# A selective-scan block with a Sinkhorn mixing tail: gate one state earlier, make-up factor 1.1, conv taps one tick later, mixing from the end of the first Sinkhorn chain

## The chip, the cores and the metric

The kernel runs on one core of one Trainium2 chip. The metric is the time of one execution on the device in microseconds (us). Each profile is one execution of the program taken by the hardware profiler. The engines are named as the profile does: PE (TensorE, matmuls; PEld its weight loads), DVE (VectorE), ACT (ScalarE), POOL (GpSimd), SP (SyncE, which issues DMAs).

## The reference

The computation is one layer with adaptive layer norms: a selective state-space block, then a residual mixing of four streams. Cut to what matters:

```python
mod = (silu(c) @ wmod)                                # six rows per batch: sa, ca, ga, sb, cb, gb
h = layernorm(x) * (1 + ca) + sa                      # x: 4 x 512 x 1024
x = x + ga * attn(h)
h = layernorm(x) * (1 + cb) + sb
x = x + gb * ffn(h)

def attn(h):                                          # DIN 2048, N 16 states, R 64, K 4
    x, z = split(h @ in_proj_w)
    xc = silu(causal_conv4(x))                        # 4 taps along the sequence
    dt_r, Bm, Cm = (rmsnorm of three slices of xc @ x_proj_w)
    dt = softplus(dt_r @ dt_proj_w + dt_bias)
    h_t = exp(dt_t * A) * h_(t-1) + dt_t * B_t * x_t  # for 2048 channels x 16 states
    y_t = sum over states of h_t * C_t
    return ((y + D * xc) * silu(z)) @ out_proj_w

def ffn(x):                                           # 4 streams of 256
    H_res = sinkhorn_log(x_norm @ W_res + base)       # 4 x 4 per position, 50 iterations
    H_res = (1 - g) * I + g * H_res
    x_pre = sum_n x_n * H_pre_n                       # H_pre, H_post: softmaxes
    return H_res @ x_streams + H_post * (x_pre @ W_branch)
```

## The kernel before

**Blocks, quads, states.** The 2,048 positions are eight blocks k of 256 (a batch and a half of it). The 2,048 channels are four quads q of four 128-channel chunks. The main loop runs over k, q and the 16 states n: 512 steps of `step`, with six ticks each. In one step VectorE runs two scans (L1160, two chunks each, `tensor_tensor_scan` along the positions) on the present state, and two sums (L1146) that add the previous state's h times C to `acc`, one for each half of the positions. ScalarE computes the decays `da` (L1125) for the next step, into the one buffer that each half has. GpSimd computes the inputs `w` (L1111, the u of the quad times B) two steps ahead, into three buffers (`emit_w`; L1116 adds the carried state in the second half of a batch). TensorE transposes the scanned states of the previous step into PSUM (`hq`, L1136, eight transposes into two banks), and does the dense products in between.

**Order.** The loops are under a manual schedule: every engine executes in the order in which the program emits. Generators (`spawn`) emit the rest of the work between the ticks: a generator that yields a number is continued that many ticks later, one that yields "v" at the next gap of VectorE (`gap`, one per tick). Dense products stand in one queue per block (`paced`): x (`product_x`, L616), z (`product_z`, L664), out (`product_out` of the block before, L845) and the projection to dt, B and C (`product_bc`, L697). At every tick the queue issues the share of its matmuls that is due; when it has been held up, it may issue at most MAKE_UP (1.2) times the pace until it has caught up.

**Convolution.** Behind the eight matmuls of a chunk, `product_x` lets ScalarE do the last tap with the bias (L625, `xc`), waits TAP_LAG (3) ticks, and gives VectorE three more taps (L632, 128 x 256 each), each in a gap of its own. The product's PSUM bank (four of the kind `mm`) is held until the last tap.

**Gate.** When a quad is done, `gate_quad` multiplies `acc` by silu(z) on GpSimd (L914, 128 x 1024), transposes the result on TensorE (L929, `py`), copies it on ScalarE into `y` (L936) and marks `done`: `product_out` waits for all four y of its block, the z product two quads on and the `acc` of the quad two on wait for the gate. It is spawned at state 2 of the next quad. Since `product_out` of a block needs the y of its quad 3, it starts in quad 0 of the next block. Its results are transposed (`pr`) and added to x on VectorE (L899, `xr`).

**Sinkhorn chains.** After block 7 the logits of 16 tiles (of 128 positions) are there, first of 14 (`early`), and of the last two (`late`, tiles 14 and 15) somewhat later. The 50 iterations are six small VectorE operations each (`iteration`, L187 to L200), with a renewal of the kernel now and then (`renew`). Chain 0 takes tiles 0 to 7 and chain 1 tiles 8 to 13; when the logits of the late tiles are ready, chain 1 takes them along (its operations become 128 wide instead of 96), noting in `behind` at which iteration. The two chains alternate operation by operation. `end` (L224, L226) writes a chain's mixing coefficients. After both ends the late tiles still lack as many iterations as chain 1 had done before they joined (`chain_late`). The branch product (x_pre @ W_branch, `branch_*`) runs on ScalarE, TensorE and GpSimd beside the chains: its last stage copies with a scale (L1317, `yn`, three buffers) and adds on GpSimd (L1319, L1320).

**Mixing.** For each of 16 tiles `mix_products` makes ten diagonal matrices on ScalarE (L1275), with which TensorE makes ten products (L1341, two instructions each in the profile): all of streams 0 and 1 (`oa`) and two of stream 2 (`ob`); ScalarE starts stream 3 (L1339). `mix_rest` adds the other five terms on VectorE (L1352), multiplies by gb (L1356, L1358), adds x1 on GpSimd (L1359) and stores (L1360). Tile i's products are emitted ahead of tile i-1's rest, and two operations of `chain_late` go between the VectorE operations of a tile; at tile 14 what is left of the chain is emitted at once.

## Time and profile before

| | us |
|---|---|
| runs (3): median, lowest, highest | 2532.35, 2531.55, 2533.06 |
| the profiled execution, its own time | 2531.71 |
| its span | 2529.9 |
| busy: PE, PEld, DVE, ACT, POOL | 2340.1, 1961.1, 2289.9, 1700.7, 1803.9 |
| granted clock of TensorE, mean | 0.965 |

The span divides into a prologue (to 126 us), eight blocks (they begin at 126, 423, 691, 960, 1231, 1498, 1766 and 2033), the end of block 7 with the chains (2292 to 2443) and the mixing (2443 to 2530). A row of the profile's groups gives the line, the engine, the operation, the tiles (out<-in) with their shapes, then the total busy time and the mean in ns of one instruction, then the idle time of the engine ahead of it and what ended it. In a timeline, a run of like instructions is one row: start and duration in us, what ran, how many, and in brackets the idle time before it with its releaser. The ends of consecutive instructions on one engine overlap by about 0.1 us, so the cost of one is its distance to the next start.

### The profile page before, as it was taken

The page shows a single profiled execution, that of the slowest core. Times are in us where ns is not written, and L with a number is a line of the kernel's source. Part 1 is how long each engine was busy: PE and PEld are TensorE (multiplying, and loading weights), DVE is VectorE, ACT ScalarE, POOL GpSimd, SP SyncE. Part 2 cuts the span into 40 slices and gives each one's busy share as a digit, 9 for nine tenths or more (in the row PEclk, how much of TensorE's full clock was granted, in tenths as well). Part 3 has the DMA queues.
Part 4 walks back from the last instruction along what each step waited for, and adds up shares of the span by engine and source line. Part 5 has one row for each costly group of instructions (what it writes and reads, how often), then busy time and mean ns, then how long its engine had stood idle before and what let it go on. Part 6 is the DMA issues. An engine that isn't in the chain of part 4 may idle for free.

```text
span 2529.9 us, 38513 instructions
## 1 busy us (share of the span) xinstructions
PE 2340.1 (92%) x13224; PEld 1961.1 (78%) x13224; DVE 2289.9 (91%) x3539; ACT 1700.7 (67%) x3775; POOL 1803.9 (71%) x1199
## 2 busy tenths in 40 slices
PE   8999989999999999999999999999999999885578
PEld 5766577888888888888788878888888877774567
DVE  2289998999899998999899999999999999988988
ACT  2366577676867686767777786768776777752466
POOL 0256567777967797878867796779676888872395
PEclk9999989999999999999999999999999999988689
DMA  7434423333423343334333433344333422323702
GB/s 263 163 117 150 148 82 134 109 129 143 142 103 123 125 163 113 115 133 145 116 124 119 150 138 109 123 149 142 104 122 109 163 100 102 115 92 111 308 19 117
DMA packets 74339, 330.98 MB, mean 131 GB/s; under 512 B 8496, under 2 KB 25312, under 8 KB 47456
## 3 DMA queue, kind: packets, MB, share of 16 engines
q1 hardware_dynamic: 62784, 311.56, 34.7%
q10 hardware_dynamic: 11360, 16.96, 1.8%
q8 instruction: 106, 1.74, 0.3%
q14 instruction: 89, 0.73, 0.1%
HBM read 303.14 MB, written 25.35 MB: 130 GB/s over the span
## 4 chain that ended last, share of the span: by engine, by line
PE 55%; DVE 25%; ACT 7%; POOL 7%; issue 5%; DMA 2%; POOLq 0%; DVEq 0%; SPq 0%; ACTq 0%
PE po L845 12%; PE pp L616 12%; PE hq L1136 11%; DVE w L1160 10%; PE pz L664 9%; DVE acc L1146 5%; POOL w L1111 3%; ACT da L1125 3%; DVE xc L632 2%; PE pm L428 2%; PE pd L774 2%; PE oa L1341 1%; PE pmr L473 1%; DMA xr<-x_dram 1%; POOL hh L979 1%
## 5 line engine op out<-in xcount | busy, mean ns | idle before, releaser
L1111 POOL TENSOR_TENSOR w<-u,b 128x1024 f32<-128x1024 f32 x512 | 1208.7, 2362 | 468.0 <-PE hq L1136 331.2
L1125 ACT ACTIVATE da<-dv,aneg 128x255 f32<-128x255 f32 x2048 | 969.1, 476 | 575.5 <-DVE w L1160 517.5
L1160 DVE TENSOR_TENSOR_SCAN w<-da,w 128x512 f32<-128x512 f32 x1024 | 1202.0, 1205 | 64.2 <-ACT da L1125 31.4
L1146 DVE SCALAR_TENSOR_TENSOR acc<-hq,ss,acc 128x512 f32<-128x512 f32 x1024 | 723.7, 736 | 49.0 <-PE hq L1136 42.5
L1136 PE MATMUL hq<-ident,w 128*128 128x128 f32 x4096 | 632.2, 279 | 65.5 <-DVE acc L1146 57.9
L1136 PEld LDWEIGHTS hq<-ident,w 128*128 128x128 f32 x4096 | 501.0, 143 | 211.8 <-issue 59.3
L664 PE MATMUL pz<-w_z,ht 128*128 128x256 f32 x2048 | 517.3, 386 | 0.0
L616 PE MATMUL pp<-ht,w_x 128*128 128x259 f32 x2048 | 505.8, 383 | 2.1 <-ACT acc L829 1.1
L845 PE MATMUL po<-y,w_out 128*128 128x256 f32 x2048 | 495.2, 380 | 0.0
L616 PEld LDWEIGHTS pp<-ht,w_x 128*128 128x128 f32 x2048 | 365.1, 190 | 49.0 <-ACT da L1125 2.6
L845 PEld LDWEIGHTS po<-y,w_out 128*128 128x128 f32 x2048 | 367.2, 190 | 39.7 <-issue 0.3
L664 PEld LDWEIGHTS pz<-w_z,ht 128*128 128x128 f32 x2048 | 366.9, 194 | 35.9 <-issue 0.7
L632 DVE SCALAR_TENSOR_TENSOR xc<-pp,cw,xc 128x256 f32<-128x256 f32 x384 | 180.8, 471 | 42.6 <-ACT xc L625 38.6
L644 POOL TENSOR_TENSOR xc<-xc,sx 128x1024 f32<-128x1024 f32 x32 | 75.6, 2364 | 43.0 <-ACT sx L642 42.8
L625 ACT ACTIVATE xc<-pp,cb,cw 128x256 f32<-128x256 f32 x128 | 71.0, 555 | 39.3 <-PE pp L616 39.0
L681 POOL TENSOR_TENSOR sz<-sz,sgz 128x512 f32<-128x512 f32 x64 | 81.6, 1276 | 2.3 <-ACT sgz L679 2.3
L806 POOL TENSOR_TENSOR u<-dv,xc 128x1024 f32<-128x1024 f32 x32 | 75.5, 2361 | 5.9 <-ACT dv L785 5.9
L979 POOL TENSOR_TENSOR hh<-hh,mrow 128x1024 f32<-128x1024 f32 x32 | 75.5, 2363 | 1.4 <-ACT hh L543 1.4
L774 PE MATMUL pd<-et,dtw 64*128 64x256 f32 x256 | 73.7, 410 | 1.2 <-DVE xr L899 0.7
L697 PE MATMUL px<-w_bc,xc 128*128 128x96 f32 x512 | 67.8, 278 | 6.4 <-POOL xc L644 6.4
L914 POOL TENSOR_TENSOR acc<-acc,sz 128x1024 f32<-128x1024 f32 x31 | 73.1, 2358 | 0.5
L697 PEld LDWEIGHTS px<-w_bc,xc 128*128 128x128 f32 x512 | 64.4, 197 | 7.7 <-POOL xc L644 7.4
(155 smaller groups left out, 2107.9 us busy)
## 6 DMA issues: line engine op xcount, KB each, us to landing
w_x<-in_w_dram SPq DMA_DIRECT2D x64, 1024.0 KB, 4.8
w_z<-in_w_dram SPq DMA_DIRECT2D x64, 1024.0 KB, 6.0
w_out<-out_w_dram SPq DMA_DIRECT2D x56, 1024.0 KB, 4.8
w_mod<-wmod_dram SPq DMA_DIRECT2D x24, 1024.0 KB, 4.9
b<-bcd SPq DMA_DIRECT2D x32, 512.0 KB, 4.4
xt<-x_dram SPq DMA_DIRECT2D x16, 512.0 KB, 6.5
xr<-x_dram SPq DMA_DIRECT2D x32, 256.0 KB, 5.1
x<-xr ACTq DMA_DIRECT2D x32, 256.0 KB
```

The costliest lines, as they stand in the source:

```text
L616: pe.matmul(pp, w[:, h, j * P : (j + 1) * P], hts[k][:, h, :], start=(h == 0), stop=(h == HC - 1),)
L632: vec.scalar_tensor_tensor(xc[:, c, :], pp[:, tap : tap + TB], cw[:, i, tap : tap + 1], xc[:, c, :], ALU.mult, ALU.add,)
L664: pe.matmul(pz[:, t, :], hts[k][:, h, PAD + t * P : PAD + (t + 1) * P], w[:, h, :], start=(h == 0), stop=(h == HC - 1),)
L697: pe.matmul(px[:, t, :], xcs[k, i // QC][:, i % QC, t * P : (t + 1) * P], xpw[:, i, :], start=(i == 0), stop=(i == DC - 1),)
L774: pe.matmul(pd[:, j, :], dtw[:, (QC * q + c) * P : (QC * q + c + 1) * P], ets[k][:R, :], start=True, stop=True,)
L845: pe.matmul(po, w[:, d - lo, :], ys[k, d // QC][:, d % QC, :], start=(d == lo), stop=(d == hi - 1),)
L979: pool.tensor_tensor(hh, hh, row, op)
L1111: pool.tensor_tensor(w, us[k, q], bts[k, n // NG][:, n % NG, :].unsqueeze(1).to_broadcast([P, QC, TB]), ALU.mult,)
L1125: act.activation(das[s][:, j, 1:], dts[k, q][:, 2 * s + j, 1:], AF.Exp, scale=aneg[:, i, n : n + 1],)
L1136: pe.transpose(h[:, c * P : (c + 1) * P], ws[g][:, c, t * P : (t + 1) * P], ident)
L1146: vec.scalar_tensor_tensor(acc[:, t, :], hqs.pop((g, t)), cts[k][:, t, n : n + 1], acc[:, t, :], ALU.mult, ALU.add,)
L1160: vec.tensor_tensor_scan(h, das[s].rearrange(row), h, 0.0, ALU.mult, ALU.add)
```

## The change

There are four edits in the main loop and the tail.

1. `gate_quad` is spawned at state 1 of the next quad instead of state 2 (the quad that `g - 2` names at state 1 is the one that `g - 3` named at state 2: the quad before).
2. MAKE_UP is 1.1 instead of 1.2.
3. TAP_LAG is 4 instead of 3 ticks.
4. When chain 0 ends, chain 1 drops the late tiles: `behind` keeps the iteration at which they joined and now also how many they have done, and `chain_late` (here the generator `rest`) alternates with what is left of chain 1, and goes on in the mixing. Tile 0's `mix_products` is emitted as soon as chain 0 has ended. Once `chain_late` is exhausted, tiles are "light": stream 2's two products on TensorE become one more copy on ScalarE and one more operation on VectorE. This holds for tiles 14 and 15. The last tile's addition of x1 is on VectorE.

```diff
-LAG, TAP_LAG, ACT_LAG, POOL_LAG, DMA_LAG = 2, 3, 5, 10, 12
-MAKE_UP = 1.2
+LAG, TAP_LAG, ACT_LAG, POOL_LAG, DMA_LAG = 2, 4, 5, 10, 12
+MAKE_UP = 1.1
...
     def chain(c):
         for it in range(SINKHORN_ITERS):
-            if c and 1 in ready and behind[0] > it:
-                behind[0] = it
-            r = slice(HALF * c, NTT if c and 1 in ready else early.stop if c else HALF)
+            if c and "half" in ready:
+                ready.add("alone")
+            joined = c and 1 in ready and "alone" not in ready
+            if joined:
+                behind[0] = min(behind[0], it)
+                behind[1] += 1
+            r = slice(HALF * c, NTT if joined else early.stop if c else HALF)
             yield from iteration(r, it)
...
     def chain_late():
-        for it in range(SINKHORN_ITERS - behind[0], SINKHORN_ITERS):
+        for it in range(behind[1], SINKHORN_ITERS):
...
+    rest = chain_late()
+
     def sinkhorn():
         chains = [chain(0), chain(1)]
-        while chains:
+        first, second = chains
+        while second in chains:
             for c in list(chains):
                 got = next(c, None)
                 if got is None:
                     chains.remove(c)
+                    if c is first:
+                        ready.add("half")
+                elif c is second and "alone" in ready and rest not in chains:
+                    chains.append(rest)
+                    yield got
                 elif got == "v":
                     yield got
...
-                    if n == 2 and g > 2:
-                        spawn(gate_quad(*where(g - 3)[:2]))
+                    if n == 1 and g > 2:
+                        spawn(gate_quad(*where(g - 2)[:2]))
...
-            on_pe = [(2, 0), (2, 1)] + [(n, m) for n in range(2) for m in range(NS)]
+            on_pe = [(n, m) for n in range(2) for m in range(NS)]
+            if not light[0]:
+                on_pe = [(2, 0), (2, 1)] + on_pe
+            lights.append(light[0])
...
-                    act.activation(ob[:, 1, :], hs[0], AF.Copy, scale=hres[:, 0, 3:4])
+                    for n3 in (2, 3) if light[0] else (3,):
+                        act.activation(
+                            ob[:, n3 - 2, :], hs[0], AF.Copy, scale=hres[:, 0, n3 : n3 + 1]
+                        )
...
-            for n, m in ((3, 1), (3, 2), (3, 3), (2, 2), (2, 3)):
+            for n, m in ((3, 1), (3, 2), (3, 3), (2, 1), (2, 2), (2, 3)):
+                if (n, m) == (2, 1) and not lights[i]:
+                    continue
...
-            pool.tensor_tensor(of, of, x1[:, i, :], ALU.add)
+            (vec if i == NTT - 1 else pool).tensor_tensor(of, of, x1[:, i, :], ALU.add)
...
+            if "half" in ready and not oas:
+                mix_products(0)
...
-            mix_products(i)
             if i:
+                mix_products(i)
                 for _ in mix_rest(i - 1):
-                    next(rest, None)
-                    next(rest, None)
+                    for _ in range(2):
+                        if next(rest, None) is None:
+                            light[0] = True
```

More of the change, by code (lines that the diff above doesn't have):

```diff
@@ L127, in adaln_block @@
     early, late = (slice(i, i + n) for i, n in parts_of)
-    ready, behind = set(), [SINKHORN_ITERS]
+    ready, behind = set(), [SINKHORN_ITERS, 0]
     def over_i(v):
@@ L263, in sinkhorn @@
                     yield from filter(None, [next(c, None)])
-                    if c is chains[0]:
+                    if c is first:
                         yield "i"
@@ L1327, in adaln_block @@
         oas, obs = {}, {}
+        light, lights = [False], []
         def mix_products(i):
@@ L1368, in adaln_block @@
                     next(branch, None)
-        rest = chain_late()
+            if "half" in ready and not oas:
+                mix_products(0)
         for i in range(NTT):
```

## The prediction

> **What bounds the kernel now.** I read four views, from coarse to fine. First the page's table of instruction groups, for the price of one instruction:

> ```profile
> L1160 DVE TENSOR_TENSOR_SCAN w<-da,w 128x512 f32<-128x512 f32 x1024 | 1202.0, 1205 | 64.2 <-ACT da L1125 31.4
> L1146 DVE SCALAR_TENSOR_TENSOR acc<-hq,ss,acc 128x512 f32<-128x512 f32 x1024 | 723.7, 736 | 49.0 <-PE hq L1136 42.5
> L632 DVE SCALAR_TENSOR_TENSOR xc<-pp,cw,xc 128x256 f32<-128x256 f32 x384 | 180.8, 471 | 42.6 <-ACT xc L625 38.6
> L914 POOL TENSOR_TENSOR acc<-acc,sz 128x1024 f32<-128x1024 f32 x31 | 73.1, 2358 | 0.5
> ```

> A step of the scan needs two scans and two sums on VectorE. In the timeline the second of two scans starts 1.13 us after the first, and two sums take 1.38 us, 0.65 from one to the next, so the shortest step is 3.5 us; with the three taps of a chunk it is 4.8.

> Then the busy time of each engine by stage (columns: window, length, then busy time with its count for PE, its weight loads, DVE, ACT and POOL; granted clock; DMA):

> ```profile
> 1498.00:1766.00 268.00, 260.30 (x1523) 224.02 (x1522) 256.60 (x325) 193.66 (x394) 217.90 (x176) 0.99 0.37 129
> 2033.00:2292.00 259.00, 234.31 (x1331) 198.22 (x1329) 237.80 (x273) 168.12 (x352) 200.54 (x164) 0.95 0.28 98
> 2443.00:2530.00 87.00, 71.91 (x320) 62.35 (x320) 72.71 (x244) 56.96 (x186) 53.67 (x23) 0.93 0.24 97
> ```

> A steady block (the first row is block 5) keeps PE busy 260.3 of 268.0 us and DVE 256.6. Both are near their limit: what is left to gain is the 11.4 us in which DVE waits. The waits of DVE over blocks 4 and 5 (1230 to 1766 us) say for whom (total, times, longest):

> ```profile
> DVE w L1160 <- ACT da L1125: 6.2, 6, 1.6
> DVE acc L1146 <- PE hq L1136: 4.9, 11, 0.6
> ```

> Last the timelines, in the place that the change touches: quad 0 of block 5, PE, then DVE, then POOL (start, duration, what ran, idle before it):

> ```profile
> 1510.57 1.22 PE L1136 MATMUL hq<-ident,w 128*128 128x128 f32 x8 [0.90 <-DVE acc L1146]
> 1515.32 1.31 PE L1136 MATMUL hq<-ident,w 128*128 128x128 f32 x8 [0.92 <-DVE acc L1146]
> 1516.48 3.62 PE L845 MATMUL po<-y,w_out 128*128 128x256 f32 x16
> ```

> ```profile
> 1529.72 0.75 DVE L1146 SCALAR_TENSOR_TENSOR acc<-hq,ss,acc 128x512 f32<-128x512 f32 x1 [0.51 <-PE hq L1136]
> 1531.04 0.75 DVE L1146 SCALAR_TENSOR_TENSOR acc<-hq,ss,acc 128x512 f32<-128x512 f32 x1 [0.56 <-PE hq L1136]
> ```

> ```profile
> 1503.94 1.28 POOL L681 TENSOR_TENSOR sz<-sz,sgz 128x512 f32<-128x512 f32 x1
> 1505.38 2.36 POOL L1111 TENSOR_TENSOR w<-u,b 128x1024 f32<-128x1024 f32 x1 [0.15 <-PE hq L1136]
> 1507.96 2.36 POOL L914 TENSOR_TENSOR acc<-acc,sz 128x1024 f32<-128x1024 f32 x1
> ```

> The reader is to see one chain. The gate (L914) runs at 1507.96; its transposes py follow at 1513.34, the copy of y at 1514.68, and only then may product_out (po) start, at 1516.48. The paced queue has nothing else to run meanwhile, so PE idles 0.90 and 0.92 us. Afterwards it makes up with 8 or 9 matmuls a step, 0.43 us each, beside eight transposes of 0.11: 4.3 to 4.8 us of PE against a 3.5-us step of DVE, and DVE waits for hq at states 6 to 11.

> **The change, part by part.** The sum is made against the profiled execution, 2531.71 us (span 2529.9, 1.81 around it); the median of the runs shown is 2532.35, 0.64 above it.

> *Gate a state sooner, and lateness made up at 1.1 times the pace.* The instruction order of the two kernels puts 27 of 31 gates ahead of the w product of state 3 instead of state 4, py and the y copies a step sooner, and po from state 2 of quad 0, at 7 a step instead of 8 or 9. Removed in quad 0 of blocks 1 to 6: the two idle stretches of PE, 0.90 + 0.92 = 1.8 us; seen from DVE, its hq waits there, .16 + .51 + .56 + .56 + .31 = 2.1 us. At 7 a step PE needs 7 x 0.43 + 0.88 = 3.9 us, 0.4 over the shortest step; over eight steps 3.2 us, less than the some 5 us that PE's two hq banks, its lead and the tapped steps absorb today (excess 0.8 to 1.3 over seven steps is 6 to 9, of which 2.1 show). I take -1.8 each, six times: -10.9; bounds 0 and -2.1 each.

> What the earlier gate costs: 2.33 us on POOL (one start to the next) ahead of w of state 3, for which the first scan of state 3 waits, and behind that scan everything on DVE. That w now ends 2.8 to 3.6 us before its scan (1508.0 against 1511.0 in the lines above), so 0.45 to 1.2 us stay as cover: nothing here. Without the cover the gate costs up to 2.33 us a time. The gate itself does not wait: the last sum of the quad before it ended 1.1 to 1.7 us earlier than POOL can begin it. PE's sequencer does not meet py before acc is ready either, as both move together.

> *Taps four ticks behind.* 111 of 384 taps come one scan later, 24 earlier. A tap that directly follows one of the same chunk takes 0.49 us to the next start, one with a scan between 0.39. Such neighbours fall from 12 to 8 a block and from some 82 to 64 in all: 18 x 0.10 = -1.8 us. The bank of the product is held a tick longer (0.6 to 0.8 us); four banks cover it.

> *The xr addition* (L899) of quad 0 now stands ahead of the second scan of state 11 in seven blocks. Its transposes on PE come only about one matmul sooner; block 4 shows what it is to meet them early, 1.68 us of wait on PE. Bounds 0 and 7 x 0.5; nearest to the other six blocks, where nothing is waited for: +1.0 in all.

> *Block 7 and block 0.* In block 7 quad 0 loses 1.3 of hq and PE idling but has 1.3 us of slack for w against 2.33, half of which shows: +0.8. Quad 3 waits 13.6 us now, of which 2.7 are hq and the last transposes; its w gets 0.3 later. Together -2.9, bounds 0 and -5. Block 0 is bound by PE in quad 3 and carries four more product matmuls there (+0.7); in quad 2 small operations of DVE that now last 2 us beside POOL's gate fall elsewhere (-0.4): +0.3.

> *The end.* The chains' end and the first tile of mixing, all engines:

> ```profile
> 2442.41 0.35 DVE L226 SCALAR_TENSOR_TENSOR z<-factors,gt,gm 128x128 f32<-128x128 f32 x1
> ...
> 2445.05 1.57 ACT L1317 ACTIVATE yn<-pb,hpp 128x256 f32<-128x256 f32 x4 [1.66 <-POOL x L1320]
> ...
> 2446.49 1.28 ACT L1275 ACTIVATE dg<-ident,z 128x128 f32<-128x128 f32 x4
> ...
> 2448.19 2.08 PE L1341 MATMUL ob<-h,dg 128*128 128x256 f32 x4 [5.60 <-ACT ob L1339]
> ...
> 2450.36 0.49 DVE L1352 SCALAR_TENSOR_TENSOR ob<-h,z,ob 128x256 f32<-128x256 f32 x1 [3.57 <-PE ob L1341]
> ```

> Chain 0's coefficients (z) are there at 2442.76, but tile 0 waits for chain 1 and for a branch copy that is held up by POOL. The change puts tile 0's diagonals ahead of both: ACT is free at 2443.4 instead of 2446.5, so ob and the first mixing operation of DVE come 3.1 us sooner, at 2447.2: -3.1, bounds -3.6 (the wait of DVE) and -1.5 (if the late chain, which now begins here too, holds DVE). The order counts 115 operations of the late chain left for mixing instead of 108, as tiles 14 and 15 leave the joined rounds two sooner; a single one between two L1352 costs nothing, a pair 0.21, I take 0.1 each: +0.6. Tiles 14 and 15 are light: DVE, the bound there, gets a sixth L1352, 2 x 0.5 = +1.0, and PE's 0.86 less per tile is worth nothing, as PE ends 3 us ahead of DVE. The last addition takes 1.23 us on DVE (L914's last instance, the same shape) instead of 2.34 on POOL, where it stands alone on the way to the output DMA: -1.15. Sum -2.65.

> [...]

> Sum: -10.9 - 1.8 + 1.0 - 2.9 + 0.3 - 2.65 = -17.0. 2531.71 - 17.0 = 2514.8, and 0.64 more for the median: **2515**.

> **Rivals.**

> *A, the waits only move.* PE is busy 97% of a steady block and does the same matmuls; DVE's waits of quad 0 may turn up two quads on, where the queue now runs late. For it: DVE waits for hq only where PE is behind. Against it: PE's own waits for DVE (7.7 us in blocks 4 and 5, half of it these two stretches) are time lost for good, and the order of the two kernels is identical from state 11 on. Then quad 0 and block 7 give nothing: -1.8 + 1.0 + 0.3 - 2.65 = -3.2, 2529.

> *B, the gate starves the scan: slower.* If the first scan of state 3 comes 1.2 us sooner against POOL than now, or the gate starts that much later, w is late at each moved gate. It decides from the point at which the gate's 2.33 us exceed the slack, 2.8 to 3.6 now. For it: 0.45 us is all that is left at some gates, z's products L681 stand ahead of the gate (1503.94), and fewer waits on DVE bring the scans forward. Against: the states ahead of the gate change little. At a lateness of 1 us, 24 gates of blocks 1 to 7 and block 0: -17 + 24 = +7, 2539.

> *C, quad 3 gains too.* 4 to 7 us of wait per block lie in quad 3 (the da and w rows of the waits). POOL and ACT take the gate's work a step sooner, when there is less behind it. Against: the order there hardly changes. At 2 us in each of blocks 1 to 6: 12 more, 2503.

> **How the numbers follow.** The forecast has 0.58, A 0.20, B 0.12, C 0.10. Its own range, from the bounds of the xr wait (-1 to +2.5), block 7 (+3 to -2), the late chain (+1.6) and quad 0 (+4 to -2), is 2508 to 2522. The range reaches up to take in A and a little of B, down to half of C: 2506 to 2532; some 0.15 stay outside. This measurement tells 0.2%, 5.06 us, from no change: faster means under 2527.3. A lies at that edge and gives 0.05 to faster, 0.14 to same and 0.01 to slower; B gives 0.10 to slower and 0.02 to same. With the forecast and C: faster 0.73, same 0.16, slower 0.11.

> **What would show it.** Right: no idle PE before hq in states 3 and 4 of quad 0, DVE's hq waits in states 6 to 11 gone, blocks 1 to 6 some 2 us shorter each, w ending 0.4 to 1.2 us before the scan of state 3, and the first L1352 (L1374 in the new numbering) 4.8 us after chain 0's last L226 begins instead of 7.9. Wrong: DVE waiting for POOL's w behind the gate (B); the same hq waits at later states (A); a wait of DVE for pr in state 11 of over 0.5 us; an output DMA that holds o's buffer, since it is issued as before but tiles come sooner.

## The result, and the profile after

The changed kernel takes 2519.43 us (median of 4 runs, 2516.47 to 2520.07) against 2532.7 (4 runs, 2531.55 to 2533.14): a ratio of 0.9943, 95% interval 0.9931 to 0.9955. The forecast was 2515: by the medians the change gained 13.3 us, where some 17 had been forecast. The profiled execution, the fastest of the four, took 2516.47, span 2514.7, which is 15.2 us under that of before. The changed kernel has other line numbers: L1173, L1159, L1149 and L1124 are L1160, L1146, L1136 and L1111 of before. By stage, from the two traces (first scan of each block, the start of chain 0's last L226, the end):

| us | before | after | difference | forecast |
|---|---|---|---|---|
| prologue | 126.5 | 127.3 | +0.8 | 0 |
| block 0 | 296.0 | 293.2 | -2.8 | +0.3 |
| blocks 1 to 6 | 1610.8 | 1600.2 | -10.6 | -11.7 |
| block 7 to chain 0's end | 409.0 | 409.8 | +0.8 | -2.9 |
| from there to the end | 87.5 | 84.2 | -3.3 | -2.65 |

The prices of single instructions, from the page's table of groups, are what they were (same columns):

```profile
L1173 DVE TENSOR_TENSOR_SCAN w<-da,w 128x512 f32<-128x512 f32 x1024 | 1203.3, 1206 | 67.5 <-ACT da L1138 34.8
L1159 DVE SCALAR_TENSOR_TENSOR acc<-hq,ss,acc 128x512 f32<-128x512 f32 x1024 | 723.4, 736 | 37.1 <-PE hq L1149 31.2
L927 POOL TENSOR_TENSOR acc<-acc,sz 128x1024 f32<-128x1024 f32 x31 | 73.1, 2357 | 0.5
```

Among the idle times, the one ahead of the sums moved most, 49.0 to 37.1 us; ahead of the scans it is 67.5 instead of 64.2. The busy time by stage (block 5, block 7, mixing; columns as before) shows PE and DVE about as full as they were in blocks 5 and 7, and DVE fuller in the mixing (75.77 of 84 us instead of 72.71 of 87):

```profile
1487.00:1756.00 269.00, 262.92 (x1539) 226.47 (x1538) 257.28 (x327) 194.16 (x394) 218.12 (x177) 0.99 0.37 129
2021.00:2280.00 259.00, 233.39 (x1326) 197.80 (x1326) 237.88 (x273) 168.24 (x350) 200.12 (x162) 0.95 0.28 97
2431.00:2515.00 84.00, 69.80 (x312) 60.17 (x312) 75.77 (x259) 56.73 (x184) 51.27 (x22) 0.93 0.25 101
```

Blocks 4 and 5 are the two that gained nothing in this execution (-0.3 and +0.1; blocks 1, 2, 3 and 6 gained 2.1 to 3.3). Their waits of DVE, for comparison with the same two lines of before:

```profile
DVE w L1173 <- ACT da L1138: 7.5, 9, 1.6
DVE acc L1159 <- PE hq L1149: 5.4, 9, 1.9
```

The wait for hq has not shrunk there, but the longest is now 1.9 us instead of 0.6. It is not in quad 0. Quad 0 of block 5, PE and then POOL and DVE:

```profile
1500.10 0.63 PE L942 MATMUL py<-ident,acc 128*128 128x128 f32 x4 [0.24 <-ACT da L1138]
1501.16 0.65 PE L942 MATMUL py<-ident,acc 128*128 128x128 f32 x4 [0.44 <-ACT hft L1013]
1501.66 1.04 PE L1149 MATMUL hq<-ident,w 128*128 128x128 f32 x8
1502.53 1.46 PE L858 MATMUL po<-y,w_out 128*128 128x256 f32 x6
```

```profile
1493.34 1.28 POOL L694 TENSOR_TENSOR sz<-sz,sgz 128x512 f32<-128x512 f32 x1
1494.57 2.37 POOL L927 TENSOR_TENSOR acc<-acc,sz 128x1024 f32<-128x1024 f32 x1
1496.89 2.37 POOL L1124 TENSOR_TENSOR w<-u,b 128x1024 f32<-128x1024 f32 x1
```

```profile
1513.62 0.75 DVE L1159 SCALAR_TENSOR_TENSOR acc<-hq,ss,acc 128x512 f32<-128x512 f32 x1 [0.56 <-PE hq L1149]
...
1533.00 1.22 DVE L1173 TENSOR_TENSOR_SCAN w<-da,w 128x512 f32<-128x512 f32 x1 [0.45 <-ACT da L1138]
```

The block begins at 1487.4. The gate runs 7.2 us into it instead of 9.9, po starts after 15.1 instead of 18.5, and the two idle stretches of 0.9 us ahead of hq are gone; 0.24 and 0.44 us ahead of py are left. The w of state 3 (1496.89) ends 1.9 us before its scan. DVE's hq waits at states 6, 7, 10 and 11 are gone; in their place stand one of 0.56 us at state 5, one for da of 0.45 us at state 10 and one of 0.28 us at state 13.

What the long wait in block 4 is: the end of its quad 3, PE, and the windows over the same time (columns as before):

```profile
1477.38 0.73 PE L837 MATMUL pa<-ident,xd 128*128 128x128 f32 x2 [0.95 <-ACT xd L825]
1479.18 0.88 PE L837 MATMUL pa<-ident,xd 128*128 128x128 f32 x2 [1.07 <-ACT xd L825]
1479.85 1.06 PE L1149 MATMUL hq<-ident,w 128*128 128x128 f32 x4
```

```profile
1478.00:1480.00 2.00, 0.93 (x4) 0.60 (x4) 1.59 (x3) 1.94 (x7) 2.00 (x3) 0.66 0.10 16
1480.00:1482.00 2.00, 2.00 (x10) 1.71 (x9) 1.55 (x3) 1.97 (x5) 2.00 (x2) 0.50 0.85 297
```

Behind two idle stretches of about 1 us the granted clock (third column from the right) is 0.50: four hq transposes take 1.06 us instead of 0.60, and DVE waits 0.45 and 1.91 us for hq. The three idle stretches alone do not decide it: in the kernel before, block 4 has the same ones (0.41, 0.94 and 1.07 us) and keeps a clock of 1.00, while block 2, with 0.42, 0.93 and 1.07, falls to 0.50 and waits 1.89 us. In the two traces the granted clock changes 82 times, in each of them only at times that are whole multiples of 3.41 us apart. In the 3.41 us up to the fall, PE was busy 1.48 us here (1475.21 to 1478.62) and 1.50 in block 2 of before (947.85 to 951.26). In block 4 of before the idle stretches lie on both sides of such a time, and PE was busy 1.99 us in the 3.41 us ahead of it and 2.27 in those behind it (1487.15 to 1490.56 to 1493.98).

The tail, all engines:

```profile
2430.47 0.35 DVE L226 SCALAR_TENSOR_TENSOR z<-factors,gt,gm 128x128 f32<-128x128 f32 x1
...
2431.60 1.28 ACT L1288 ACTIVATE dg<-ident,z 128x128 f32<-128x128 f32 x4
...
2433.30 1.13 PE L1361 MATMUL ob<-h,dg 128*128 128x256 f32 x4 [2.65 <-ACT ob L1357]
...
2435.11 0.49 DVE L1374 SCALAR_TENSOR_TENSOR ob<-h,z,ob 128x256 f32<-128x256 f32 x1 [0.19 <-ACT dg L1288]
```

The first L1374 begins 4.64 us after chain 0's last L226 instead of 7.95. The first ob is at full clock (1.13 us for its four matmuls, granted clock 1.00 from 2433.30 to 2434.36), and DVE is now held by the chains' own operations up to 0.19 us before it.

### The profile page after: what moved, and what is told of

It is laid out like the page before. It is cut to its first block, busy times and chain, and to the rows that moved or that the text cites. A ratio compares the mean times of both kernels' runs of the same rounds, so it can differ in the third digit from the quotient of the medians.

```text
span 2514.7 us, 38529 instructions
## 1 busy us (share of the span) xinstructions
PE 2333.1 (93%) x13216; PEld 1954.6 (78%) x13216; DVE 2287.9 (91%) x3554; ACT 1700.2 (68%) x3773; POOL 1800.6 (72%) x1198
## 4 chain that ended last, share of the span: by engine, by line
PE 48%; DVE 26%; ACT 10%; POOL 8%; issue 6%; DMA 2%; SPq 0%; DVEq 0%; POOLq 0%; ACTq 0%
DVE w L1173 12%; PE po L858 10%; PE pp L629 10%; PE hq L1149 9%; PE pz L677 8%; DVE acc L1159 5%; POOL w L1124 4%; ACT da L1138 4%; DVE xc L645 2%; PE pm L441 2%; PE oa L1361 1%; PE pmr L486 1%; DMA xr<-x_dram 1%; PE pd L787 1%; PE plg L1020 1%
## 5 line engine op out<-in xcount | busy, mean ns | idle before, releaser
L1124 POOL TENSOR_TENSOR w<-u,b 128x1024 f32<-128x1024 f32 x512 | 1208.6, 2362 | 455.7 <-PE hq L1149 307.1
L1173 DVE TENSOR_TENSOR_SCAN w<-da,w 128x512 f32<-128x512 f32 x1024 | 1203.3, 1206 | 67.5 <-ACT da L1138 34.8
L1159 DVE SCALAR_TENSOR_TENSOR acc<-hq,ss,acc 128x512 f32<-128x512 f32 x1024 | 723.4, 736 | 37.1 <-PE hq L1149 31.2
L1149 PE MATMUL hq<-ident,w 128*128 128x128 f32 x4096 | 628.8, 278 | 55.8 <-DVE acc L1159 48.6
L1149 PEld LDWEIGHTS hq<-ident,w 128*128 128x128 f32 x4096 | 499.5, 143 | 199.2 <-issue 60.3
L858 PE MATMUL po<-y,w_out 128*128 128x256 f32 x2048 | 502.0, 381 | 0.0
L819 POOL TENSOR_TENSOR u<-dv,xc 128x1024 f32<-128x1024 f32 x32 | 75.6, 2361 | 5.9 <-ACT dv L798 5.9
L927 POOL TENSOR_TENSOR acc<-acc,sz 128x1024 f32<-128x1024 f32 x31 | 73.1, 2357 | 0.5
```

The lines of the kernel that those rows point to most:

```text
L858: pe.matmul(po, w[:, d - lo, :], ys[k, d // QC][:, d % QC, :], start=(d == lo), stop=(d == hi - 1),)
L1124: pool.tensor_tensor(w, us[k, q], bts[k, n // NG][:, n % NG, :].unsqueeze(1).to_broadcast([P, QC, TB]), ALU.mult,)
L1149: pe.transpose(h[:, c * P : (c + 1) * P], ws[g][:, c, t * P : (t + 1) * P], ident)
L1159: vec.scalar_tensor_tensor(acc[:, t, :], hqs.pop((g, t)), cts[k][:, t, n : n + 1], acc[:, t, :], ALU.mult, ALU.add,)
L1173: vec.tensor_tensor_scan(h, das[s].rearrange(row), h, 0.0, ALU.mult, ALU.add)
```

## The experiments

Every kernel was timed in five rounds beside the kernel before on the same chip, which gave a median of 2533.32 in the first set, 2533.51 in the second, 2535.43 in the third and 2532.39 in the last. The stages are those of each one's profiled execution.

| kernel | median, us | ratio to before, 95% interval | block 0 | blocks 1 to 6 | block 7 to chain 0's end | to the end |
|---|---|---|---|---|---|---|
| before | 2532.7 | | 296.0 | 1610.8 | 409.0 | 87.5 |
| after | 2519.43 | 0.9943 (0.9931 to 0.9955) | 293.2 | 1600.2 | 409.8 | 84.2 |
| x1 gate alone | 2526.47 | 0.9962 (0.9950 to 0.9975) | 297.5 | 1604.3 | 408.3 | 87.7 |
| x2 MAKE_UP 1.1 alone | 2538.57 | 1.0016 (1.0007 to 1.0025) | 294.8 | 1615.3 | 411.7 | 90.6 |
| x3 taps alone | 2530.16 | 0.9982 (0.9973 to 0.9990) | 296.7 | 1609.0 | 410.8 | 86.8 |
| x4 tail alone | 2528.61 | 0.9973 (0.9961 to 0.9985) | 294.8 | 1610.0 | 408.9 | 83.7 |
| x5 gate and MAKE_UP | 2528.62 | 0.9981 (0.9972 to 0.9991) | 295.2 | 1602.7 | 410.6 | 87.3 |
| x6 after, gate of block 7 as before | 2520.72 | 0.9945 (0.9932 to 0.9959) | 293.8 | 1599.9 | 409.7 | 85.8 |
| x7 after, no light tiles | 2517.01 | 0.9932 (0.9919 to 0.9945) | 292.9 | 1602.8 | 410.2 | 83.3 |
| x8 after, idle transposes | 2516.58 | 0.9931 (0.9917 to 0.9945) | 292.3 | 1600.0 | 409.8 | 84.2 |
| x9 after, MAKE_UP 1.2 | 2520.32 | 0.9944 (0.9932 to 0.9956) | 298.2 | 1600.9 | 410.0 | 83.9 |
| x10 after, 1.2 in block 7 | 2516.53 | 0.9932 (0.9918 to 0.9945) | 293.7 | 1603.0 | 410.3 | 84.0 |
| x11 x7, x8, x10 and more | 2514.3 | 0.9922 (0.9910 to 0.9935) | 292.3 | 1601.2 | 409.3 | 82.7 |
| x12 x11, clock kept up in block 7 | 2515.5 | 0.9922 (0.9909 to 0.9936) | 293.0 | 1601.8 | 410.4 | 82.2 |

The stages scatter: up to block 6 x6, x7 and x10 run the same loop as the changed kernel, and their blocks 1 to 6 lie from 0.3 us under to 2.8 us over it. In the total none of x6 to x10 is told apart from the changed kernel.

**x1 to x4: each part alone, on the kernel before.** x1 is the hunk of `gate_quad`, x4 all that concerns `chain`, `chain_late`, `sinkhorn` and the mixing; x2 and x3 are the constants:

```diff
-MAKE_UP = 1.2
+MAKE_UP = 1.1
...
-LAG, TAP_LAG, ACT_LAG, POOL_LAG, DMA_LAG = 2, 3, 5, 10, 12
+LAG, TAP_LAG, ACT_LAG, POOL_LAG, DMA_LAG = 2, 4, 5, 10, 12
```

> The kernel before with the gate a state earlier, nothing else. Theory (the late start of product_out is what costs quad 0): PE's two idle stretches of 0.9 us go, so quad 0 of blocks 1 to 6 gets about 1.2 to 1.8 us shorter each, while DVE's hq waits stay as the make-up at 1.2 is unchanged; in all -7 to -11, 2522 to 2526, with block 7 giving nothing. Rival (the size of the make-up is what costs): the gate alone gives under -4, 2529 or more.

> The kernel before with MAKE_UP 1.1, nothing else. Theory: PE's idle stretches in states 3 and 4 stay, the backlog is made up over more steps; -0 to -3, 2529.5 to 2532.5. Rival (the make-up is what costs): DVE's hq waits at states 6 to 11 go, -2 in each of six blocks, about 2520.

> The kernel before with TAP_LAG 4, nothing else. Theory (fewer neighbouring taps): 18 pairs times 0.10 us, -1.8, spread over quads 0 to 2, 2530.8. Rival (a tap that comes later also spares waits for ScalarE's first tap, or moves sums so that PE is ready): quad 1 of blocks 1 to 6, which got 0.6 us shorter with the whole change, shows this here too, -3 to -5, 2528. If quad 1 stays as it was, its gain came from the paced queue.

> The kernel before with the edits from the Sinkhorn chains on, nothing else; the main loop is the old one. Theory: all of the tail's gain is its own: from the last L226 of chain 0 to the end 84.2 us instead of 87.5, so -3.3, about 2529.3. Rival (the clock and the state of the engines at the end of block 7 decide the tail): -1 or less.

The gate alone gave -6.9 us, at the edge of what the theory asked. Blocks 1 to 6 are 6.5 us shorter: quad 0 by 4.2, quad 1 by 3.3 and quad 3 by 1.6, while quad 2 is 2.7 us longer. There DVE waits 4.2 us ahead of the xr addition, instead of 1.7. The edit also removed DVE's hq waits at states 7, 10 and 11 of quad 0, which the theory had left to MAKE_UP. MAKE_UP 1.1 alone is slower, outside both expectations. Quad 0 of block 5 in x2, DVE:

```profile
1549.98 0.75 DVE L1146 SCALAR_TENSOR_TENSOR acc<-hq,ss,acc 128x512 f32<-128x512 f32 x1 [1.09 <-PE hq L1136]
1552.11 0.75 DVE L1146 SCALAR_TENSOR_TENSOR acc<-hq,ss,acc 128x512 f32<-128x512 f32 x1 [1.38 <-PE hq L1136]
```

With a late gate a slower make-up carries the backlog on to state 11, where stage_dt's matmuls come in ahead of the next hq, and DVE waits 2.5 us in each of these blocks. It costs a second time at the end: 88 instead of 72 instructions of product_out are left after the last gate, the logits of the late tiles come 5.4 us later, so these join chain 1 later, and 132 instead of 120 small chain operations follow the first L1352 (75.6 us from there to the last tile instead of 72.4). The taps gave -3.2, between theory and rival; in the trace blocks 1 to 6 are 1.8 us shorter. Quad 1 of these blocks became only 1.0 us shorter together, against 3.3 with the gate alone, although six taps moved from it into quad 2; so the gain of quad 1 in x1 came from the paced queue. The tail kept its gain by itself: 83.7 us from chain 0's last L226 instead of 87.5.

**x5 and x9: MAKE_UP with the early gate.** x5 is x1 with 1.1; x9 is the changed kernel with 1.2.

> The kernel before with the gate a state earlier and MAKE_UP 1.1 together; the earlier gate alone gave -7, the slower make-up alone +5. If the two add up, -2: 2531. Theory (the slower make-up is harmful only where the backlog is large; with the earlier gate it is small, and then it spares DVE the hq waits): better than the gate alone, -8 to -11, 2522 to 2525, and no hq wait of over 0.5 us left in quad 0 of blocks 1 to 6; the waits of 1.08 and 1.38 us at state 11, which the slower make-up alone has, are absent.

> The changed kernel with MAKE_UP back at 1.2. The two experiments on it so far disagree with the change: 1.1 alone cost 5 us, and on top of the earlier gate it gained nothing. Theory (with the gate early the backlog is small; 1.1 spares DVE about 1.4 us of hq waits in quad 0 over six blocks, but in block 7 it leaves five matmuls of product_out to the end, where PE alone sets the time): quad 0 of blocks 1 to 6 +1 to +2 together, from block 7's start to the end of chain 0 -2; in all 2518 to 2520, no difference. Rival (1.1 is harmful throughout): 2515 or less. Second rival (1.1 belongs to the gain): 2522 or more.

The waits at state 11 are absent in x5, as expected (of the hq waits in quad 0, 0.56 us at state 5 is the longest left), but it is not better than x1, and outside the 2522 to 2525 that were expected. Its quad 0 of blocks 1 to 6 is 5.5 us shorter than before and its quad 2 is 5.0 longer: DVE waits there 3.1 us ahead of xr and 3.3 for hq at states 13 and 14, where before it waited 1.7 and nothing. In x9 blocks 1 to 6 are within 0.7 us of the changed kernel, and DVE idles as long in quad 0 (13.1 us in six blocks, 13.0 after; 19.4 before). So with the early gate and the later taps the make-up factor is worth nothing there. Where it shows is block 0: quad 3 takes 68.8 to 70.1 us in the five kernels with 1.2 there and 67.6 to 67.9 in all with 1.1. Added up by the medians, the gate and MAKE_UP together (x5, -4.9), the taps (-3.2) and the tail (-4.7) make -12.8, near the -13.3 of the whole change; x1 to x4 one by one make -9.5, as MAKE_UP alone costs 5.3.

**x6 and x10: block 7.** Each is the changed kernel with one edit of its main loop, the first x6, the second x10:

```diff
-                    if n == 1 and g > 2:
-                        spawn(gate_quad(*where(g - 2)[:2]))
+                    back = 3 if k == NBLK - 1 else 2
+                    if n == back - 1 and g > back:
+                        spawn(gate_quad(*where(g - back)[:2]))
```

```diff
-                    room = min(room + MAKE_UP * rate, 1.5 * TB)
+                    room = min(room + up * rate, 1.5 * TB)
...
-                pace = paced(columns[k])
+                pace = paced(columns[k], 1.2 if k == NBLK - 1 else MAKE_UP)
```

> The changed kernel with the gate back at state 2 in block 7 alone. Theory (there POOL has no slack, and the gate delays w of state 3): the waits of DVE for w at state 3 of 1.24 us (quad 0) and 2.84 us (quad 3) go; in quad 0 DVE gets about 1 us back, in quad 3 the same 3 us come back at states 3 to 5 as before. Quads 0 and 3 of block 7 together 0.5 to 1.5 us shorter, the total -1, 2518. Rival (something else lengthened block 7): quad 0 stays at 62.7 us or longer.

> The changed kernel with 1.2 in block 7 alone, 1.1 in all others. Theory (the end of block 7 is PE's: matmuls of product_out that are left over when the scan ends add their 0.43 us each to the chain of gate, product_out, logits; DVE's waits in block 7 are covered by it): none left instead of five, so from block 7's start to the end of chain 0 409.8 - 5 x 0.43 = 407.7 us, the total -2, 2517. Rival (DVE sets the end of block 7): 409.8 or more, as quad 3's waits for hq grow.

In x6 the wait for w behind the gate went, and quads 0 and 3 of block 7 (quad 3 up to its state 15) became 2.5 and 2.1 us shorter (60.1 and 62.8 us), more than expected; quad 1 became 1.8 longer. Yet chain 0 ends as late: DVE is through its last sum at 255.3 us of the block instead of 258.2, and the last matmul of product_out comes at 280.3 instead of 280.4, as 88 instructions are left behind the gate instead of 74. PE's end of product_out, first in the changed kernel (block 7 begins at 2020.7), then in x6 (at 2021.3):

```profile
2280.34 1.57 PE L942 MATMUL py<-ident,acc 128*128 128x128 f32 x8 [2.42 <-DVE acc L927]
...
2299.63 1.46 PE L858 MATMUL po<-y,w_out 128*128 128x256 f32 x6
```

```profile
2300.13 1.46 PE L858 MATMUL po<-y,w_out 128*128 128x256 f32 x6
```

Between the first and the last matmul of product_out behind the gate PE is busy 19.36 of 19.39 us in the changed kernel, and 21.77 of 21.90 in x6. In x10 only 64 are left, the least there can be, but quad 3 takes 68.0 us instead of 65.0 and the last matmul comes at 282.1. So neither theory holds alone: what DVE gains PE has still to do, and what PE does earlier DVE waits for.

**x7: light tiles.**

```diff
-                            light[0] = True
+                            light[0] = False
```

> The changed kernel without light tiles: tiles 14 and 15 keep ten products on PE and five operations on DVE. Theory (DVE is the bound at the end, PE has room): from the first mixing operation on DVE to the last tile's L1380 73.57 - 2 x 0.5 = 72.6 us; total -1. Rival (PE sets the pace of the last tiles, which is what light tiles are for): the same or up to +1.7.

From the first L1374 to the last L1380 72.62 us instead of 73.57, as the theory had it: light tiles cost 0.95 us.

**x8: the clock.**

```diff
                 pa = bank(f"pa_{k}_{q}_{t}", (P, QC * P))
+                if q == 0 or NQ * k + q == NBLK * NQ - 1:
+                    for c in range(8):
+                        pe.transpose(pa[:, c % QC * P : (c % QC + 1) * P], ident, ident)
```

> The changed kernel with eight idle transposes of the identity ahead of each of the two acc transposes in the last states of quad 3 (and of quad 2 in block 7), into the bank that the real ones then overwrite: some 0.9 us of PE work each where PE waits 0.9 and 1.1 us for xd. Theory (the granted clock falls to 0.5 in some blocks after these idle stretches, and DVE then waits for hq at states 14 and 15; whether a given block is hit varies from run to run): the granted clock stays at 1.00 at the end of quad 3 in blocks 1 to 6, the waits of 0.45 + 1.9 us are gone, and the time falls by 2 to 5 us with less scatter, 2514 to 2517. Rival (the clock does not matter there, or the fill delays hq itself): the same or up to +5.

Partly. In blocks 1 to 6 the time at half clock adds up to 24 us in the changed kernel (27, 31 and 34 in x6, x7 and x10, which run the same main loop there) and to 10 in x8, in three stretches of 3.4 us: two in quad 2, behind PE's waits for the projection, where nothing was filled, and one in quad 3 of block 2 (944 to 948 us, at 0.54 and 0.61), in which the fill itself takes 1.9 us and DVE waits 2.1 us for hq. The median is 2.9 us under that of the changed kernel, but the two intervals overlap and the scatter (2514.47 to 2521.4) did not shrink.

**x11: the versions together**, with eight more idle transposes ahead of product_bc in each block but block 0.

> What the runs point to, together: the changed kernel without light tiles (-1), with the idle transposes ahead of the acc transposes (-2 to -3) and eight more ahead of each block's projection product (product_bc), where PE waits 1.2 and 0.3 to 0.6 us for POOL and ScalarE and the clock fell to 0.5 behind it in about one block in six, and with 1.2 in block 7 (-2). Theory: they add up, 2512 to 2514, from block 7's start to the end of chain 0 about 407.7 us, mixing 72.6, and no stretch at half clock in blocks 1 to 6. Rival (the fill takes PE time that blocks 1 to 6 lack, as PE is busy 97%): 2516 or more, quads 2 and 3 longer than the 68.0 to 68.9 and 65.0 to 66.0 us they take undisturbed.

At 2514.3 us (five runs, 2513.56 to 2515.72) it is below every run of the changed kernel, and the fastest measured. Theory and rival each hold in part: mixing takes 71.6 us and every run shows a granted clock of 0.973 (0.966 to 0.968 for the changed kernel), but three stretches of 3.4 us at half clock are left in blocks 1 to 6 (in quad 3 of blocks 2 and 4, and in block 5), blocks 1 to 6 are not shorter in its profiled execution, and block 7 gave 0.5 us instead of 2. In quad 2 the clock of the changed kernel had fallen to 0.50 behind PE's waits for the projection in two of these six blocks (3 and 5, at 1140.7 and 1676.6 us), not in one; in x11 it is 1.00 around these waits in all six. In the mixing 6 fewer operations of the late chain are left than in x7, whose mixing takes 72.62 us. So the idle transposes hold the clock up; that the gain over the changed kernel comes from it, beyond the 0.95 us of the light tiles, is not shown.

**x12: the clock in block 7.** This is x11 with one more edit:

```diff
                 hqs[g, t] = h
+                if LAST - N <= g + 1 < LAST - N + 4:
+                    for c in range(2 * QC):
+                        pe.transpose(h[:, c % QC * P : (c % QC + 1) * P], ident, ident)
```

> The previous version (no light tiles, idle transposes, 1.2 in block 7) with eight more idle transposes ahead of each half's transposes hq in states 0 to 3 of block 7's quad 3, where PE waits 1.2, 2.6, 1.6 and 2.4 us for DVE and POOL and the granted clock is 0.50 to 0.63 for some 15 us. Theory (the half clock there costs DVE its hq waits and PE the first matmuls of product_out behind the gate, and the end of block 7 is PE's): granted clock over 0.9 from 2206 to 2221 us, from block 7's start to the end of chain 0 406 to 407.5 us instead of 409.3, the total 2511 to 2513. Rival (POOL's queue ahead of the gate sets this stretch): 409 or more, no difference in the total.

The windows of PE (window, length, busy time, granted clock, DMA) in x11, then in x12:

```profile
2206.00:2211.00 5.00, 1.94 (x8) 0.63 0.00 0
2211.00:2216.00 5.00, 1.94 (x8) 0.50 0.01 2
2216.00:2221.00 5.00, 4.80 (x20) 0.50 0.02 3
```

```profile
2210.00:2215.00 5.00, 2.89 (x17) 0.77 0.02 3
2215.00:2220.00 5.00, 4.52 (x36) 0.89 0.01 2
2220.00:2225.00 5.00, 4.60 (x37) 1.00 0.00 0
```

The clock is higher, if not over 0.9 throughout as expected, and nothing was gained: block 7 to chain 0's end 410.4 us. Quad 3 is 0.5 us shorter up to its state 15, but the fill also brings a wait of 1.05 us for hq at state 1, and quads 0 and 2 came out 1.5 and 0.6 us longer in this execution. The rival holds for the total; that POOL's queue sets this stretch was not tried.

## Why the prediction was right, point by point

- **Gate and make-up, blocks 1 to 6 quad 0: forecast -10.9, measured -7.5,** and -5.5 in x5, which has just these two edits. The mechanism was right: the two idle stretches of PE went and so did the hq waits of DVE, and x1 shows that the gate does it. The size was off: "I take -1.8 each" left out that a queue which starts sooner also makes new waits; those at states 5, 10 and 13 take back some 1.2 us a block (DVE's idle time in these six quads fell by 6.4 us). And the reasoning on 7 matmuls a step was idle: at 8 or 9 a step the early gate does the same (x9).
- **Quads 1 and 2 were left out of the sum.** In six blocks quad 1 gained 3.8 us and quad 2 lost 1.8. The two belong together: with TAP_LAG 4 one tap a block comes in quad 2 instead of quad 1 (2.6 us of busy time in all). In x1 and x5, where no tap moves, quad 1 gains 3.3 and 3.4 us and quad 2 loses 2.7 and 5.0, to waits of DVE.
- **The gate's cost: nothing, confirmed** in blocks 1 to 6. Behind the moved gates the w of state 3 still ends 0.8 to 4.4 us before its scan there, where 0.45 to 1.2 was forecast, so rival B's point was not reached. In block 7 it was: DVE waits 1.24 us for w behind the gate in quad 0, which became 0.8 us longer, as forecast. In quad 3 it waits 2.84 us at state 3, in place of 3.07 at states 3 to 5.
- **Taps: -1.8 by pairs.** Neighbouring taps fell from 83 to 64 as counted ahead. Alone the edit leaves 75, which by the forecast's 0.10 us a pair is 0.8 us, and gave 3.2 us by the medians (ratio 0.9982). Where the rest of that comes from stays open.
- **The xr addition: forecast +1.0.** It did not come: in quad 0 the wait of block 4 fell from 1.68 to 0.73 us, and blocks 1 to 3, 5 and 6 wait for nothing there, before and after. Waits ahead of xr grew in quad 2 of x1 and x5, which the forecast left out.
- **Block 7: forecast -2.9, measured +0.8: the step that failed.** "Quad 3 waits 13.6 us now" counted waits of DVE as time on the path. In the changed kernel DVE is through its last sum 0.1 us sooner in the block than before, and the last matmul of product_out comes 1.6 us later: two more instructions are left behind the gate, and the granted clock there is 0.94 on the mean, where it was 1.00. x6 brings DVE's last sum 2.9 us forward, and chain 0 ends at the same time, as PE is busy without a break behind the gate.
- **Block 0: forecast +0.3, measured -2.8.** Most of it is in the PE-bound quad 3 (-2.5), where the forecast saw only four more matmuls. Set beside the kernels with 1.2 and 1.1 in the experiments, MAKE_UP is worth 0.9 to 2.5 us there.
- **Tail: forecast -2.65, measured -3.3**: -3.31 up to the first L1374 (-3.1), +1.18 for the late chain and the light tiles together (+1.6), -1.16 at the last addition (-1.15). The first ob came at full clock after 2.65 us of idling (1.13 us); in the kernel before, ob took 2.08 us after 5.60, and four like matmuls (L1311, at 2409.12) 2.07 us after 2.52, both at a granted clock of 0.50. The clock fell after the change too, at 2434.4, just behind ob, to 0.50 for 3.41 us: PE had been busy 1.06 us in the 3.41 us up to there, and 1.26 us in the 3.41 us up to the fall at 2408.8 of the kernel before, ahead of those four. That the fall came just behind ob and not ahead of it was not forecast, and what decides it is not shown. The tail hardly gained by it, as DVE was busy with the chains until 0.19 us before its first operation on ob.
- **Rivals.** A (the waits only move) holds for a third of the forecast for quad 0, for quad 2 of x1 and x5, which is "two quads on", and for block 7. C fell: quad 3 of blocks 1 to 6 kept 34.4 us of DVE's idle time, of 34.8.

That the sum came so near is in part luck, as the misses cancel. Quad 0 and block 7 gave 7.1 us less than forecast, and the prologue was 0.8 longer; block 0 gave 3.1 more, the other quads of blocks 1 to 6 gave 2.3 more (-3.1, where taps and xr were to make -0.8), and the tail 0.6 more. By the medians the forecast was 4.4 us too low.

## What to carry to other kernels

Where two engines are both near their limit, idle time of the one that precedes a burst of waits of the other is the place to look: start the late producer sooner, rather than stretch the make-up. A setting that helps in one arrangement (a slower make-up) can cost when it stands alone, so test a bundle's parts one by one and then in pairs. Before counting a wait as a gain, ask what the next stage waits for: in the last block what one engine gained the other had still to do.
